# The sums of two group norms: VectorE's reductions, or matmuls with the values as weights

## The chip, the cores and the metric

The kernel runs on one core of one Trainium2 chip. The metric is device time in microseconds of one execution, from the runs' times; a profiled execution of the same kernel gives the trace. Engines have these names: PE is TensorE's matmul, PEld its weight load, DVE is VectorE, ACT is ScalarE, POOL is GpSimd, SP is the engine that issues the DMAs.

## The reference

For each of 16 samples (256 channels, 32 x 32 positions, f32), two layers are applied, each to a group norm of what came before, and each with a residual:

```python
    def _gn(v, G=16, eps=1e-5):
        B_, H_, W_, C_ = v.shape
        g = v.reshape(B_, H_, W_, G, C_ // G)
        m = jnp.mean(g, axis=(1, 2, 4), keepdims=True)
        s = jnp.var(g, axis=(1, 2, 4), keepdims=True)
        return ((g - m) / jnp.sqrt(s + eps)).reshape(v.shape)
    ...
    x = x + _L0_conv_ref(_gn(x), ...)
    x = x + _L1_conv_ref(_gn(x), ...)
```

The array given to `_gn` has the shape (16, 256, 32, 32). The norm takes its last axis, 32 wide, as channels: a group is two neighbouring columns of the 32 x 32 picture, over all 256 channels and all 32 rows, 16,384 numbers. There are 16 groups in a sample. Layer 0 is an attention block (4 heads of 32 on 1024 tokens, layer norms, a feed-forward part). Layer 1 is a gated state-space scan: 512 inner channels, 64 states each, a recurrence over 1024 steps, with projections, a short convolution and gates around it.

## The kernel before

**Layout.** A sample is held as two tiles of 128 channels x 1024 tokens, channels on the partitions. So a group of the norm is a set of columns, the same on each partition: column c belongs to group (c mod 32) // 2. A sum over a group needs a sum over columns within a partition and a sum over all partitions.

**The loop.** The recurrence is cut into units. A unit is one scan instruction on DVE (L922, 128 x 1024), and a sample has 256 of them (4 x 4 x 2 x 8), 4096 in all. With the scan of unit n the loop issues, in this order: the DMA that brings the operand `dub` of unit n + 6; POOL's product with `bt` for unit n + 4 (L905); a piece of `outputs` of the last block of eight units (PE L947 with 32 passes in a unit, ACT's copy L953 in every second one, PE L959 with 64 small passes and ACT's copy L963 in every eighth); the scan; `decay` of unit n + 2 (two PE matmuls L914 into a PSUM tile, then ACT's exponential L916 in place). The pool of decay tiles has two buffers, so a decay can be at most two units ahead. All engines work in program order, and the end of the kernel ties that order down for PE, ACT, DVE and POOL.

**The side work.** All else for the next sample (`first_norm`, `attention_layer`, `scan_inputs`) and the last step for the sample before (`gate_and_store`) is written as generators. After the decay of a unit, the loop takes as many steps from them as are due. A step yields its share; `rate_for` finds a rate so that a sample's shares, each at least one unit long if it is one or more, fill 247 units. A step with share 1.5 is thus followed by a pause of the larger of 1 and 1.5 / rate units. The shares of a sample add up to 271.9 where `gate_and_store` runs too. Sample 0 is prepared ahead of the loop, with no scan beside it, and the last 256 units have no sample to prepare.

**The norm.** `group_norm` (L258) is called twice for a sample: in `first_norm` (L360), in the first units of a sample's 256, and in `scan_inputs` (L610), some 160 units later. `sum_of` (L259) reduces a tile of 1024 columns to 16 sums on DVE (L261). `mean_of` (L263) adds the two tiles' sums over the partitions on PE with a matrix of 1/256 (L266), which leaves the result on every partition. DVE scales it (L278), subtracts it from both tiles (L280), and ACT squares them (L282). The same sums of the squares give the variance, on which ACT takes Ln and Exp (L291, L292; Ln takes the scale in), and DVE multiplies (L295). PSUM tiles of side work come from `psum`, two buffers in the pool `mm` while the scan runs.

Other lines that are spoken of: L435 is the attention's scores for the maxima, L445 a reduction of 64 columns, L465 the attention's values `v_ps` (128 x 128 f32 pieces of `xn` as weights), L491 and L503 the matmuls of the value stage, 32 steps of share 1.75 in a sample.

Of the kernel before, what the change touches and what calls it, by code (L numbers as in the profile page):

```python
# [11 lines left out]
F32 = mybir.dt.float32  # L12
BF16 = mybir.dt.bfloat16
AF = mybir.ActivationFunctionType
ALU = mybir.AluOpType
AX = mybir.AxisListType
# [3 lines left out]
P = 128  # L20
C = 256
KC = C // P
L = 1024
HL = 512
NG = 16
HEADS, DH = 4, 32
INNER = HEADS * DH
NJ = L // P
# [22 lines left out]
def attention_then_scan_kernel(  # L51
# [18 lines left out]
    nc = tc.nc  # L70
    B = x.shape[0]

    def pool(name, bufs, **kw):
        return ctx.enter_context(tc.tile_pool(name=name, bufs=bufs, **kw))

    const = pool("const", 1)
# [4 lines left out]
    small = pool("small", 2)  # L81
# [14 lines left out]
    def bank(src, name):  # L96
        return src.tile([P, HL], F32, name=name, tag="mm" if src is mm else "av")

    def free_bank(name):
        if spare:  # L100
            return spare.pop()
        if next(alone) is mm:
            return bank(mm, name)
        both = aps.tile([P, L], F32, name=name, tag="a")
        spare.append(both[:, hs(1)])
        return both[:, hs(0)]

    def psum(name, dims=P):
        return (bank(mm, name) if beside["scan"] else free_bank(name))[:dims]
# [7 lines left out]
    def work(name, n=L):  # L117
        return wide.tile([P, L + 2 + CONV], F32, name=name, tag="wide")[:, :n]
# [21 lines left out]
    ident = const.tile([P, P], F32, name="ident")  # L140
    make_identity(nc, ident)
    avg = const.tile([P, P], F32, name="avg")
    nc.vector.memset(avg, 1.0 / C)
    eps = const.tile([P, 1], F32, name="eps")
    nc.vector.memset(eps, 1e-5)

# [15 lines left out]
    for k in range(ND):  # L162
# [4 lines left out]
        for j in range(2):  # L167
# [3 lines left out]
                start=(j == 0), stop=(j == 1),  # L171
# [32 lines left out]
    t = work("ones_s")[:1]  # L204
# [3 lines left out]
    for k in range(KC):  # L208
        t = work("rel_s").rearrange("p (i j) -> p i j", j=32)
# [37 lines left out]
    def grouped(ap):  # L247
        return ap.rearrange("p (h g t) -> p h g t", g=NG, t=2)

    def over_group(s):  # L250
        return s.unsqueeze(1).unsqueeze(3).to_broadcast([P, L // (2 * NG), NG, 2])
# [4 lines left out]


    def group_norm(src, dst):  # L258
        def sum_of(part, s, k):  # L259
            view = part.rearrange("p (h g t) -> p g h t", g=NG, t=2)  # L260
            nc.vector.tensor_reduce(s[:, k, :], view, AX.XY, ALU.add)  # L261

        def mean_of(s, name):  # L263
            m = psum(f"{name}_ps")[:, :NG]
            for k in range(KC):
                nc.tensor.matmul(m, avg, s[:, k, :], start=(k == 0), stop=(k == KC - 1))  # L266
            return m

        per = C / (C * L / NG)
        s = small.tile([P, KC, NG], F32, name="gn_s", tag="gn_s")  # L270
        sum_of(src[0], s, 0)
        yield 1
        sum_of(src[1], s, 1)
        m = mean_of(s, "gn_m")
        yield 1
        s = small.tile([P, KC, NG], F32, name="gn_q", tag="gn_s")
        qs = []
        nc.vector.tensor_scalar(m, m, per, None, ALU.mult)  # L278
        for k in range(KC):
            nc.vector.tensor_tensor(grouped(dst[k]), grouped(src[k]), over_group(m), ALU.subtract)  # L280
            q = work("gn_sq")
            nc.scalar.activation(q, dst[k], AF.Square)  # L282
            qs.append(q)
            yield 1
        sum_of(qs[0], s, 0)
        yield 1
        sum_of(qs[1], s, 1)
        del qs, q
        v = mean_of(s, "gn_v")
        yield 1  # L290
        nc.scalar.activation(v, v, AF.Ln, bias=eps, scale=per)  # L291
        nc.scalar.activation(v, v, AF.Exp, scale=-0.5)  # L292
        yield 2.2
        for k in range(KC):
            nc.vector.tensor_tensor(grouped(dst[k]), grouped(dst[k]), over_group(v), ALU.mult)  # L295
            yield 0.6
# [53 lines left out]
    def first_norm(b):  # L350
        xs, tok = [], []
        kept = state[b]["kept"] = dram.tile([C, L], F32, name="kept", tag="kept")
        if "x" in state[b]:
            xs = state[b].pop("x")
        else:
            for go in fetches(xs, x[b]):
                go()
            yield 0.4
        gn = [work("gn") for _ in range(KC)]
        yield from along(group_norm(xs, gn), fetches(tok, pos))  # L360
        for k in range(KC):
            nc.vector.tensor_tensor(tok[k], tok[k], gn[k], ALU.add)
            nc.sync.dma_start(kept[ts(k, P), :], tok[k])
            yield 0.6
# [231 lines left out]
    def scan_inputs(b):  # L596
# [8 lines left out]
        for t in xp:  # L605
            nc.vector.memset(t[:, 0:1], 0.0)
            nc.vector.memset(t[:, L + 1 : L + 2], 0.0)
        rels = []
        yield from along(
            group_norm(xs, body),  # L610
            [partial(nc.sync.dma_start, st["xr"][ts(k, P), :], xs[k]) for k in range(KC)]
            + fetches(rels, rel) + bring,
# [387 lines left out]
    for n, (b, k, q, e, i) in enumerate(units):  # L1000
        at = n % UNITS
        if at == 0:
            parts = [prepare(b + 1)] if b + 1 < B else []
            total = steps * len(parts)
            if b > 0:
# [3 lines left out]
                total = total + GATE  # L1009
# [104 lines left out]
```

## Time and profile before

| | us |
|---|---|
| median of 3 runs | 13106.57 |
| lowest, highest | 13067.61, 13129.75 |
| the profiled execution | 13096.86 |
| its span, first to last instruction | 13095.1 |
| DVE busy | 11666.7 |
| POOL busy | 9815.4 |
| PE busy, PEld busy | 9717.3, 5456.0 |
| ACT busy | 7520.3 |
| DVE's scans L922 | 9215.1 |
| mean granted TensorE clock | 0.800 |

A row of the groups reads: line, engine, operation, output <- input by the program's names, shapes, count | busy us, mean ns of one | idle time of the engine ahead of them, and what ended most of it. The timeline gives start, length, engine, line and operation, with like neighbours merged and counted. An f32 matmul of the program stands as two matmul rows (passes) in the trace. A busy PE is not PE at its peak: matmuls overlap, and their ends are modelled.

### The profile page before, as it was taken

The numbers are of one execution on the slowest core, as the hardware profiler recorded it, in microseconds if no ns is written. First come the engines' busy times: TensorE is split into PE (matmuls) and PEld (weight loads), VectorE is DVE, ScalarE is ACT, GpSimd is POOL, SyncE is SP. The second block draws the span as 40 slices with busy tenths as digits, with TensorE's granted clock in tenths as the row PEclk, the third lists the DMA queues.
The fourth block names the chain that finished last, engine by engine and source line by source line (L and its number), as shares of the span: only waits on it lengthen the run. The fifth ranks groups of instructions, "written<-read, shape, count | busy, mean of one in ns | idle before, by whom it ended". The sixth has DMA issues, their size and how long they took to land.

```text
span 13095.1 us, 424083 instructions
## 1 busy us (share of the span) xinstructions
PE 9717.3 (74%) x186800; PEld 5456.0 (42%) x186800; DVE 11666.7 (89%) x7560; ACT 7520.3 (57%) x10421; POOL 9815.4 (75%) x4105
## 2 busy tenths in 40 slices
PE   6676876868778687786868767687686877868767
PEld 2344443444444344443444434444344444444445
DVE  3789999899999899988999898999989899889998
ACT  2465664655646556565665656566465664655654
POOL 0487876878778787786877768787687877878798
PEclk8887977879788697887879878797787977869755
DMA  1467666676666767666666666766667666676676
GB/s 52 165 220 238 208 218 218 220 243 201 221 216 219 235 200 233 216 220 231 211 224 218 213 223 213 236 210 219 218 218 234 205 218 217 218 236 204 227 248 231
DMA packets 1038401, 2820.10 MB, mean 215 GB/s; under 512 B 290370, under 2 KB 368451, under 8 KB 1036548
## 3 DMA queue, kind: packets, MB, share of 16 engines
q1 hardware_dynamic: 1036548, 2792.97, 64.6%
q8 instruction: 1459, 23.90, 0.7%
q14 instruction: 394, 3.23, 0.1%
HBM read 2513.82 MB, written 261.62 MB: 212 GB/s over the span
## 4 chain that ended last, share of the span: by engine, by line
DVE 36%; PE 31%; issue 13%; ACT 11%; DMA 6%; POOL 2%; SPq 1%; DVEq 0%; POOLq 0%; ACTq 0%
DVE h L922 25%; PE yb L947 6%; ACT a L916 5%; DVE mx L416 5%; PE a L914 5%; PE av L491 3%; PE g_ps L688 2%; DMA dub<-dus 2%; PE st_ps L503 2%; POOL dub L905 2%; PE z_ps L639 2%; PE yb L959 1%; PE m_ps L859 1%; PE qk_ps L403 1%; DVE u L674 1%
## 5 line engine op out<-in xcount | busy, mean ns | idle before, releaser
L905 POOL TENSOR_TENSOR dub<-dub,bt 128x1024 f32<-128x1024 f32 x4096 | 9810.6, 2417 | 3229.8 <-DMA dub<-dus 2896.6
L922 DVE TENSOR_TENSOR_SCAN h<-a,dub 128x1024 f32<-128x1024 f32 x4096 | 9215.1, 2278 | 752.0 <-ACT a L916 401.8
L916 ACT ACTIVATE a<-a,acol 128x1024 f32<-128x1024 f32 x4096 | 4462.8, 1090 | 3253.4 <-PE a L914 3206.7
L914 PE MATMUL a<-pieces,pick 48*128 48x512 bf16 x8192 | 1902.6, 455 | 2518.2 <-DVE h L922 2401.8
L947 PEld LDWEIGHTS yb<-h,cd 128*32 128x32 f32 x131072 | 2488.2, 128 | 2781.3 <-issue 1265.6
L947 PE MATMUL yb<-h,cd 128*32 128x64 f32 x131072 | 3255.8, 252 | 476.8 <-ACT y L953 325.2
L914 PEld LDWEIGHTS <-pick 48*128 48x128 bf16 x8192 | 603.3, 95 | 2915.4 <-issue 2467.5
L953 ACT COPY y<-yb 128x256 f32<-128x256 f32 x2048 | 763.6, 373 | 914.7 <-PE yb L947 907.5
L435 PE MATMUL s_ps<-k,q 32*64 32x512 f32 x4092 | 825.7, 619 | 95.5 <-DVE mx L416 95.0
L416 DVE TENSOR_REDUCE mx<-s_ps 128x1 f32<-128x512 f32 x1023 | 649.0, 681 | 15.5 <-PE s_ps L435 15.5
L491 PE MATMUL av<-pt,vv 128*64 128x512 f32 x2048 | 596.1, 662 | 3.0 <-ACT sums L480 1.7
L959 PE MATMUL yb<-turn,y 128*32 128x16 f32 x32768 | 591.4, 214 | 5.8 <-issue 4.9
L511 ACT ACTIVATE pt<-st_ps 128x512 f32<-128x512 f32 x1024 | 554.1, 599 | 60.9 <-PE st_ps L503 59.9
L959 PEld LDWEIGHTS yb<-turn,y 128*32 128x32 f32 x32768 | 573.8, 159 | 6.6 <-issue 5.2
L503 PE MATMUL st_ps<-sp 33*128 33x512 f32 x2048 | 561.8, 622 | 4.5 <-ACT pt L511 3.3
L963 ACT COPY yo<-yb 128x128 f32<-128x128 f32 x512 | 136.1, 266 | 587.8 <-PE yb L959 560.5
L688 PE MATMUL g_ps<-w,xp 128*128 128x256 f32 x1464 | 451.9, 447 | 0.0
L688 PEld LDWEIGHTS g_ps<-w,xp 128*128 128x128 f32 x1464 | 367.3, 326 | 65.5 <-issue 54.0
L435 PEld LDWEIGHTS s_ps<-k,q 32*64 32x64 f32 x4092 | 193.6, 131 | 440.8 <-DVE mx L416 421.1
L859 PE MATMUL m_ps<-w,xs 128*128 128x256 f32 x1024 | 317.5, 460 | 10.4 <-DVE xs L834 10.4
L674 DVE SCALAR_TENSOR_TENSOR u<-up,cwh,u 128x1024 f32<-128x1024 f32 x192 | 273.0, 1422 | 28.0 <-ACT u L666 27.7
L859 PEld LDWEIGHTS m_ps<-w,xs 128*128 128x128 f32 x1024 | 262.1, 328 | 55.9 <-issue 32.0
(177 smaller groups left out, 6690.8 us busy)
## 6 DMA issues: line engine op xcount, KB each, us to landing
dub<-dus SPq DMA_DIRECT2D x4096, 512.0 KB
dps<-pc SPq DMA_DIRECT2D x384, 128.0 KB
pieces<-dps SPq DMA_DIRECT2D x1024, 48.0 KB
xs<-in_x_dram SPq DMA_DIRECT2D x64, 512.0 KB
xs<-kept SPq DMA_DIRECT2D x64, 512.0 KB
zs<-z SPq DMA_DIRECT2D x64, 512.0 KB
ud<-u SPq DMA_DIRECT2D x64, 512.0 KB
dus<-du SPq DMA_DIRECT2D x64, 512.0 KB
```

The costliest lines, as they stand in the source:

```text
L416: nc.vector.tensor_reduce(mx[:, g, c, hf : hf + 1], s, AX.X, ALU.max)
L435: nc.tensor.matmul(waiting[g][0][ts(e, 64)], q4[r, ts(c, 64)], k4[r, hs(hf)], start=True, stop=True,)
L491: nc.tensor.matmul(av[ts(e, 2 * DH)], vv[j // (NJ // 2)][:, j % (NJ // 2), 2 * pair + e, :], pts[e], start=(j == 0), stop=(j == NJ - 1),)
L503: nc.tensor.matmul(s, ka[r, ts(j, P)], qa[r, hs(hf)], start=True, stop=True)
L688: nc.tensor.matmul(ps[:, ts(q, C)], xp[k][:, ds(first + t, P, 4)], wg_s[:, k, t, :], start=(k == 0 and t == 0), stop=False,)
L905: nc.gpsimd.tensor_tensor(v, v, blocks[units[n][0]]["bt"], ALU.mult)
L914: nc.tensor.matmul(a[:, hs(hf)], w, pieces[r], start=True, stop=True)
L916: nc.scalar.activation(a, a, AF.Exp, scale=acol[:, at : at + 1])
L922: nc.vector.tensor_tensor_scan(now["h", e][:, i, :], decays.pop(n), loaded.pop(n), 0.0, ALU.mult, ALU.add)
L947: nc.tensor.matmul(yb[ts(g, 32), ts(s, 64)], cd[:, at // 16, ts(c, 32)], hbuf[:, :, at : at + 8], start=(c == 0), stop=(c == 1),)
L953: nc.scalar.copy(y2[:, r], yb[:, :256])
L959: nc.tensor.matmul(some[ts(r, 32), x], y2[:, r, x:256:8], turn[:, x], start=True, stop=True)
```

## The change

The sum over the partitions comes first, and the sum over the columns second. `sum_of` issues eight matmuls on PE for a tile: 128 columns of values are the weights (128 x 128, f32), a column of ones is the moving side, and the result is one PSUM column with a sum over 128 channels for each of these 128 tokens. Two tiles give 16 such columns. `mean_of` reduces the 16 columns to one on DVE; now partition p holds the sum of all columns c with c mod 128 = p. A constant matrix `member` (128 x 16, 1/16384 where p belongs to the group) is multiplied by it, and one matmul with a matrix of ones brings the 16 means to every partition. The scalings of the mean and inside Ln fall away, since `member` holds them. Three constants are built ahead of the loop. Each half of a sum becomes a step of share 1.5, and `mean_of` a step of its own.

```diff
@@ -141,6 +141,15 @@
+    column = const.tile([P, 1], F32, name="column")
+    nc.vector.memset(column, 1.0)
+    every = const.tile([P, P], F32, name="every")
+    nc.vector.memset(every, 1.0)
+    member = const.tile([P, NG], F32, name="member")
+    nc.vector.tensor_reduce(
+        member, ident.rearrange("p (h g t) -> p g h t", g=NG, t=2), AX.XY, ALU.add
+    )
+    nc.vector.tensor_scalar(member, member, 1.0 / (C * L / NG), None, ALU.mult)
...
     def group_norm(src, dst):
-        def sum_of(part, s, k):
-            view = part.rearrange("p (h g t) -> p g h t", g=NG, t=2)
-            nc.vector.tensor_reduce(s[:, k, :], view, AX.XY, ALU.add)
-
-        def mean_of(s, name):
+        def sum_of(part, sums, k):
+            for j in range(NJ):
+                at = k * NJ + j
+                nc.tensor.matmul(
+                    sums[:, at : at + 1], part[:, ts(j, P)], column, start=True, stop=True
+                )
+
+        def mean_of(sums, name):
+            total = small.tile([P, 1], F32, name="gn_t", tag="gn_t")
+            nc.vector.tensor_reduce(total, sums, AX.X, ALU.add)
+            share = small.tile([P, NG], F32, name="gn_g", tag="gn_g")
+            nc.vector.tensor_scalar(share, member, total, None, ALU.mult)
             m = psum(f"{name}_ps")[:, :NG]
-            for k in range(KC):
-                nc.tensor.matmul(m, avg, s[:, k, :], start=(k == 0), stop=(k == KC - 1))
+            nc.tensor.matmul(m, every, share, start=True, stop=True)
             return m
 
-        per = C / (C * L / NG)
-        s = small.tile([P, KC, NG], F32, name="gn_s", tag="gn_s")
+        s = psum("gn_sum")[:, : KC * NJ]
         sum_of(src[0], s, 0)
-        yield 1
+        yield 1.5
         sum_of(src[1], s, 1)
+        yield 1.5
         m = mean_of(s, "gn_m")
         yield 1
-        s = small.tile([P, KC, NG], F32, name="gn_q", tag="gn_s")
         qs = []
-        nc.vector.tensor_scalar(m, m, per, None, ALU.mult)
...
+        s = psum("gn_sum")[:, : KC * NJ]
         sum_of(qs[0], s, 0)
-        yield 1
+        yield 1.5
         sum_of(qs[1], s, 1)
         del qs, q
+        yield 1.5
         v = mean_of(s, "gn_v")
         yield 1
-        nc.scalar.activation(v, v, AF.Ln, bias=eps, scale=per)
+        nc.scalar.activation(v, v, AF.Ln, bias=eps)
```

## The prediction

> **What bounds the kernel now.** I read the page first, its busy times and its chain.
>
> ```profile
> PE 9717.3 (74%) x186800; PEld 5456.0 (42%) x186800; DVE 11666.7 (89%) x7560; ACT 7520.3 (57%) x10421; POOL 9815.4 (75%) x4105
> ...
> DVE 36%; PE 31%; issue 13%; ACT 11%; DMA 6%; POOL 2%; SPq 1%; DVEq 0%; POOLq 0%; ACTq 0%
> ```
>
> VectorE is the fullest engine (89%, idle for 1428 us), but PE holds nearly as much of the chain. So the loop has to be read unit by unit (a unit: one scan and what is issued with it), in the stage that changes. Next the groups by line, shapes kept apart:
>
> ```profile
> L261 DVE TENSOR_REDUCE gn_q<-gn_sq 128x16 f32<-128x1024 f32 x64 | 76.4, 1196 | 0.0
> L261 DVE TENSOR_REDUCE gn_s<-xs 128x16 f32<-128x1024 f32 x64 | 75.8, 1204 | 7.1 <-DMA xs<-in_x_dram 7.1
> L266 PE MATMUL gn_m_ps<-gn_s,avg 128*128 128x16 f32 x128 | 37.6, 377 | 34.8 <-DVE gn_s L261 34.8
> L278 DVE TENSOR_SCALAR gn_m_ps<-gn_m_ps 128x16 f32<-128x16 f32 x32 | 5.3, 165 | 1.2 <-PE gn_m_ps L266 1.2
> ```
>
> The change removes the first two rows: 152.2 us, 1.2% of the span. It is little, so what comes in its place decides. The timeline of VectorE in a second norm:
>
> ```profile
> 12145.16 2.28 DVE L922 TENSOR_TENSOR_SCAN h<-a,dub 128x1024 f32<-128x1024 f32 x1
> 12147.35 1.19 DVE L261 TENSOR_REDUCE gn_s<-xs 128x16 f32<-128x1024 f32 x1
> 12148.46 2.28 DVE L922 TENSOR_TENSOR_SCAN h<-a,dub 128x1024 f32<-128x1024 f32 x1
> 12150.66 0.16 DVE L278 TENSOR_SCALAR gn_m_ps<-gn_m_ps 128x16 f32<-128x16 f32 x1
> ...
> 12161.92 6.64 DVE L922 TENSOR_TENSOR_SCAN h<-a,dub 128x1024 f32<-128x1024 f32 x3
> ```
>
> VectorE has no gap here: a unit with a reduction takes 3.30 us (12145.16 to 12148.46), three scans in a row take 6.64, so 2.21 each, and a reduction costs 1.1 us of the path, not 1.2. Last, PE in the same form as the new matmuls: v_ps (L465) has 128x128 f32 values as weights. Each f32 matmul is two passes in the trace (L465: 8 calls, 16 rows).
>
> ```profile
> 2287.34 0.61 PE L914 MATMUL a<-pieces,pick 48*128 48x512 bf16 x2 [0.56 <-DVE h L922]
> 2287.88 3.78 PE L465 MATMUL v_ps<-w,xn 128*128 128x128 f32 x16
> 2291.59 1.08 PE L947 MATMUL yb<-h,cd 128*32 128x64 f32 x32
> 2292.61 0.60 PE L914 MATMUL a<-pieces,pick 48*128 48x512 bf16 x2
> ...
> 2294.07 2.05 PE L465 MATMUL v_ps<-w,xn 128*128 128x128 f32 x16
> ```
>
> The same 16 passes take 3.78 us and 2.05 us. The windows tell why: the granted clock was 0.50 in the first and 1.00 in the second. And in the norms:
>
> ```profile
> 3095.00:3215.00 120.00, 107.38 (x2230) 51.24 (x2221) 106.40 (x48) 96.03 (x148) 109.94 (x48) 0.97 0.72 237
> 2818.00:2850.00 32.00, 15.26 (x278) 10.04 (x281) 29.79 (x18) 17.27 (x22) 32.00 (x15) 0.50 0.74 252
> 3311.00:3322.00 11.00, 7.86 (x180) 4.98 (x176) 11.00 (x13) 5.09 (x7) 4.45 (x3) 0.78 0.85 279
> 3322.00:3334.00 12.00, 6.13 (x137) 4.07 (x137) 11.97 (x9) 5.96 (x8) 10.53 (x5) 0.50 0.89 311
> ```
>
> (Columns: window, its length, busy us of PE, PEld, DVE, ACT, POOL, then clock, DMA share, GB/s.) The first is the attention's value stage, the second a first norm, the others a second norm. In the first norm, and in the second one from its 11th microsecond on, PE is busy for half of the time and at half clock.
>
> **The change part by part.** Two norms for each of 16 samples, two sums in each: 64 pairs of half-sums. Four pairs run in the prologue, 60 beside scans.
>
> Removed on VectorE: two reductions a pair, 2 x 1.1 = 2.2 us, 60 x 2.2 = 132 us, and 30 scalings L278 at 0.19 us (12150.66 to 12150.85), 6 us. Added on VectorE: in each pair a reduction of 16 columns and a scaling of 16, which no row has; L278's 0.16 bounds one from below, the reduction of 64 columns L445 (220 ns) from above: 0.36 for both, 22 us. If nothing waited, 132 + 6 - 22 = 116 us would be gained, 0.9%.
>
> Added on PE: 8 matmuls, 16 passes a half-sum, each with its own weights. The moving column is one wide; no row has that. From above L465 bounds it (0.213 us a pass at half clock, 3.4 us a half-sum; 0.112 and 1.8 at full). L266, with 16 columns and equal weights, is nearest: four passes take 1.17 us in 12148.03 to 12149.20, and a pair's ends there lie 0.21 us apart at half clock, as far as L465's. So a narrow moving side gains nothing: the weights set the pace. From below the 32-column passes of L947 (32 in 0.84 us) would give 0.42 us a half-sum. I take L465's pace, as L266 agrees.
>
> Who is behind these passes? PE's queue is in order: outputs of the last block (1.0 us at half clock), decay of the scan two units ahead (0.54), then the side step. A decay stuck behind a half-sum makes ACT's exponential late and then the scan; only two decays are ahead. From the end of a scan, at half clock (S0, S1 the two half-sums): decay 0.54, S0, outputs 1.0, decay 0.54, S1. VectorE, after two more scans (4.4), reaches the new small reduction and waits for S1: 0.3 to the end of the last pass (3.78 less 16 x 0.213 = 3.4, rounded down), 0.36 for both small operations. Behind it in VectorE's queue stand the next scans (two, 4.4), and POOL's buffers come free with these; the fourth one's decay is ready about then (outputs 1.0, then 1.75 from L914's start to the end of L916's exponential). The mean's matmul waits on PE for the small operations, with one matmul where there were two; the outputs and the decay of that unit are ahead of it, so nothing is late for it. The four scans end at 0.54 + 1.0 + 0.54 + 0.3 + 0.36 + 4.4 + S0 + S1 = 7.1 + S0 + S1. Before: 4 x 2.21 + 2.2 + 0.2 = 11.2. **The balance** is S0 + S1 = 4.1 us, 0.13 us a pass; the two measured paces, 0.112 and 0.213, lie on both sides of it. At full clock the first terms shrink to 6.6 and S0 + S1 = 3.5: 1.1 us gained a pair. At half clock 6.8: 2.7 lost. With one half-sum at each, 5.2: 1.1 lost.
>
> Which clock? L465 itself began at 0.50 and kept it for 3.3 us of dense passes; the next dense stretch, 3 us later, had 1.00. So I take the first half-sum at half clock and the second at full for the two pairs of a first norm and the second pair of a second norm (45 pairs, +1.1 each, 50 us). The first pair of a second norm has 0.78 already: near the balance, -0.3 each, 15 pairs, -5. **Sums: +45 us.**
>
> The Trainium skill (TensorE: Matmul & The Clock Gate, Part 1) says the clock is released after a busy window of about 3.4 us and falls back after an idle one, which fits the L465 rows; it does not say whether loading weights alone counts as busy. The same page (LDWEIGHTS) gives columns/1.2 ns, 107 ns for 128 columns, with no word of the clock; the L465 rows show that only at full clock. By that rule, as an estimate, S0 + S1 would be 3.4 us everywhere and the sums 0.7 us a pair, 42 us, faster.
>
> Moved: the step shares. A norm's shares grow by 4, so a batch's go from 271.9 to 279.9 in 247 units, and the rate from 1.179 to 1.238 (my working from the code). Steps of share 1.75 then come every 1.414 units instead of 1.484: 32 such in the value stage, 2.25 units fewer. That stage is full on all sides (107.4 PE, 109.9 POOL, 106.4 DVE of 120 us). A unit fewer takes 2.21 us of scan away but only 0.97 of PE (0.47 + 0.5 at full clock): 0 to 2.25 x 1.24 = 2.8 us a batch, I take 1.4, over 15 batches **+21 us** (0 to 42). In stages that VectorE fills, the denser steps cost nothing. The DMAs in the norms come with the same steps, at most a unit later, and are needed many units later: nothing.
>
> Prologue: the second half-sum can't start before its tile (25.38 us) and no scan hides it: 2 to 3.4 against 1.2 in four pairs, **+8 us**, with setup under 1.
>
> Sum: 45 + 21 + 8 = 74 on the profiled execution's 13096.9 (span 13095.1), which lies 10 us under the median of the runs, 13106.6: **13180**.
>
> **The rivals.**
> *Half clock throughout.* Passes with one column may not count as work for the clock; the norms' windows now stand at 0.50. 60 x 2.7 = 162, value stage 42, prologue 10, and up to 20 where the 64 small passes of L959 (1.17 us) follow a sum: 234 at most, 13340. Against: L465's change of clock.
> *Faster: full clock throughout.* If the passes keep to 0.11 us in all pairs, the decays are late by less than the removed reductions: 60 x -1.1 = -66, with nothing lost in the value stage and 4 in the prologue: 13045. At the pace of L947 it would be all of 116: 12990. It decides below 0.13 us a pass. Against: the windows at 0.50.
> *POOL and DMA set the pace.* In the second norm DMA is at 0.85 to 0.89 and POOL once waits 4.58 us for dub; in the first one POOL runs without a gap (32.00 of 32.00). If the scans wait there for POOL anyway, the sums cost 0, the value stage 10 and the prologue 8: 13125. Against: the timeline of the second norm, in which no scan waits for POOL.
>
> **How the numbers follow.** Forecast 0.40 (its own range 13130 to 13235), half clock 0.28, full clock 0.10, POOL and DMA 0.22. About 0.5% (13041 to 13172) is what a measurement of this kernel can tell from no change. Under it lies most of full clock: 0.08. Over it: half clock, and over half of the forecast: 0.51. The rest, 0.41, is within. The range goes from full clock's end, 13040, to 13345.
>
> **What would show it.** Right: L261's 1.2 us rows gone; 2048 passes in place of 256, 16 of them in 3.4 us where the clock is 0.50 and 1.8 where it is 1.00; the small reduction waiting 2 to 4 us for PE; more of the scan's wait for ACT's a; VectorE less busy by some 130 us and idle longer by more. Wrong: passes under 0.1 us at half clock, or scans that follow each other without a gap behind the sums; or a norm's stage that is as long as before while another stage has grown.

## The result, and the profile after

The changed kernel takes 20625.79 us (median of 4 runs, 20617.16 to 20649.53) against 13093.89 us (4 runs, 13067.61 to 13129.75) for the kernel before on the same chip: a ratio of 1.5752, with a 95% interval of 1.5716 to 1.5789. The prediction was 13180, with a range that ended at 13345. It was wrong, and not by a term of its sum: something happened that the sum did not hold.

The page of the changed kernel, with its busy times, its chain and the row of the scan (which was L922 and is L937 now; the lines below the norm have moved by 15):

```profile
PE 11861.3 (58%) x188720; PEld 6578.0 (32%) x188720; DVE 12059.0 (58%) x7532; ACT 7641.5 (37%) x10421; POOL 9771.5 (47%) x4105
...
DVE 42%; PE 32%; ACT 16%; issue 7%; DMA 1%; POOL 0%; DVEq 0%; SPq 0%; ACTq 0%; POOLq 0%
...
L937 DVE TENSOR_TENSOR_SCAN h<-a,dub 128x1024 f32<-128x1024 f32 x4096 | 9369.7, 2288 | 5512.4 <-ACT a L931 4639.0
```

The scans themselves are as long as before (2288 ns against 2278). What is new is the idle time ahead of them: 5512.4 us, and 4639.0 of it ended with ACT's `a`, the decay. The row of before:

```profile
L922 DVE TENSOR_TENSOR_SCAN h<-a,dub 128x1024 f32<-128x1024 f32 x4096 | 9215.1, 2278 | 752.0 <-ACT a L916 401.8 <-PE yb L947 156.3 <-POOL dub L905 110.6
```

So the idle time was 752.0 us there. The waits, as what waited for what, us in total, times and the longest, say who waits for whom:

```profile
ACT a L931 <- PE a L929: 9437.1, 3635, 7.6
...
PE a L929 <- DVE h L937: 8484.8, 3471, 15.5
...
DVE h L937 <- ACT a L931: 4639.0, 2663, 4.2
```

It is a ring: the exponential waits for PE's decay, the scan for the exponential, and PE's next decay for the scan (8484.8 us in 3471 waits). The timeline shows it best where nothing else runs. In this stretch of the last sample's units there is no side work and no sum, and still:

```profile
19704.07 2.29 DVE L937 TENSOR_TENSOR_SCAN h<-a,dub 128x1024 f32<-128x1024 f32 x1 [1.89 <-ACT a L931]
...
19706.41 0.61 PE L929 MATMUL a<-pieces,pick 48*128 48x512 bf16 x2 [2.56 <-DVE h L937]
...
19707.06 1.09 ACT L931 ACTIVATE a<-a,acol 128x1024 f32<-128x1024 f32 x1 [3.09 <-PE a L929]
...
19708.25 2.29 DVE L937 TENSOR_TENSOR_SCAN h<-a,dub 128x1024 f32<-128x1024 f32 x1 [1.89 <-ACT a L931]
```

The decay's matmul starts when a scan ends, the exponential follows it, and the next scan follows that: 4.18 us from scan to scan (19708.25 less 19704.07), 2.29 of scan and 1.89 of waiting. No decay is made ahead. The same place of the kernel before:

```profile
12595.59 17.91 DVE L922 TENSOR_TENSOR_SCAN h<-a,dub 128x1024 f32<-128x1024 f32 x8
```

Eight scans in 17.91 us, 2.24 each, with no gap. So units without a norm became slower too; no sum stands beside them that could do this. A second thing is seen in the sums themselves. The variance of the prologue's second norm, in the timeline and then in the windows (window, its length, busy us of PE, PEld, DVE, ACT, POOL, clock, DMA share, GB/s):

```profile
292.45 6.99 PE L271 MATMUL gn_sum<-column,gn_sq 128*128 128x1 f32 x32 [2.41 <-ACT gn_sq L295]
```

```profile
292.50:299.40 6.90, 6.90 (x32) 6.85 (x32) 0.00 (x0) 2.34 (x2) 0.00 (x0) 0.50 0.71 275
```

32 passes in 6.99 us, 0.218 each, back to back with PE busy for all of it, and the granted clock stays at 0.50 from end to end. The prediction expected it to be released in such a stretch.

The removed rows of 1.2 us are gone; in their place stand these two (the groups by line, shapes kept apart):

```profile
L279 DVE TENSOR_SCALAR gn_g<-member,gn_t 128x16 f32<-128x16 f32 x64 | 67.0, 1048 | 2.3
...
L277 DVE TENSOR_REDUCE gn_t<-gn_sum 128x1 f32<-128x16 f32 x63 | 10.7, 169 | 237.4 <-PE gn_sum L271 237.3
```

The reduction of 16 columns costs 0.17 us, but VectorE waits 237 us ahead of it. The scaling of 128x16 numbers costs 1.05 us, where the prediction took 0.36 for both operations.

**Where the decay tile went.** In the prologue, before any scan runs, `psum` takes its tiles from `free_bank`. It gives out a bank of `mm`, then the first half of a tile from the pool of decay tiles, then the second half of the same tile, which it keeps in the list `spare` until it is asked for: a cycle of three requests. Following the code, the kernel before makes 193 such requests in the prologue, 64 cycles and one: the list is empty when the loop begins. The change makes two more in each norm (`psum("gn_sum")`, where the sums had been in SBUF), four in the prologue: 197, 65 cycles and two. The last request takes a first half, and the second one stays in `spare`. Nobody asks for it as long as the loop runs, and so one of the two decay tiles stays taken.

### The profile page after: what moved, and what is told of

Read it like the earlier page. It is cut to its first block, busy times and chain, and to the rows that moved or that the text cites. A ratio compares the mean times of both kernels' runs of the same rounds, so it can differ in the third digit from the quotient of the medians.

```text
span 20615.4 us, 427971 instructions
## 1 busy us (share of the span) xinstructions
PE 11861.3 (58%) x188720; PEld 6578.0 (32%) x188720; DVE 12059.0 (58%) x7532; ACT 7641.5 (37%) x10421; POOL 9771.5 (47%) x4105
## 4 chain that ended last, share of the span: by engine, by line
DVE 42%; PE 32%; ACT 16%; issue 7%; DMA 1%; POOL 0%; DVEq 0%; SPq 0%; ACTq 0%; POOLq 0%
DVE h L937 37%; ACT a L931 13%; PE a L929 10%; PE s_ps L450 4%; PE yb L962 3%; PE av L506 3%; PE st_ps L518 2%; DVE mx L431 2%; PE gn_sum L271 2%; PE u_ps L675 1%; PE g_ps L703 1%; PE z_ps L654 1%; PE yb L974 1%; DMA dub<-dus 1%; PE m_ps L874 1%
## 5 line engine op out<-in xcount | busy, mean ns | idle before, releaser
L937 DVE TENSOR_TENSOR_SCAN h<-a,dub 128x1024 f32<-128x1024 f32 x4096 | 9369.7, 2288 | 5512.4 <-ACT a L931 4639.0
L929 PE MATMUL a<-pieces,pick 48*128 48x512 bf16 x8192 | 2181.6, 520 | 8566.8 <-DVE h L937 8484.8
L962 PEld LDWEIGHTS yb<-h,cd 128*32 128x32 f32 x131072 | 2954.5, 147 | 3068.6 <-issue 1963.6
L962 PE MATMUL yb<-h,cd 128*32 128x64 f32 x131072 | 3811.3, 282 | 42.3 <-ACT y L968 38.5
L929 PEld LDWEIGHTS <-pick 48*128 48x128 bf16 x8192 | 692.4, 97 | 9049.5 <-issue 7501.8
L450 PE MATMUL s_ps<-k,q 32*64 32x512 f32 x4096 | 912.0, 979 | 17.4 <-DVE mx L431 17.4
L506 PE MATMUL av<-pt,vv 128*64 128x512 f32 x2048 | 825.7, 897 | 2.8 <-ACT sums L495 1.6
L518 PE MATMUL st_ps<-sp 33*128 33x512 f32 x2046 | 805.2, 870 | 2.0 <-ACT pt L526 2.0
L675 PE MATMUL u_ps<-xp,w 128*128 128x512 f32 x508 | 353.0, 833 | 4.1 <-ACT u L681 4.1
L784 DVE SCALAR_TENSOR_TENSOR d_ps<-sp_s,d_ps 128x512 f32<-128x512 f32 x128 | 89.2, 697 | 382.8 <-ACT d_ps L780 382.8
```

The lines of the kernel that those rows point to most:

```text
L450: nc.tensor.matmul(waiting[g][0][ts(e, 64)], q4[r, ts(c, 64)], k4[r, hs(hf)], start=True, stop=True,)
L506: nc.tensor.matmul(av[ts(e, 2 * DH)], vv[j // (NJ // 2)][:, j % (NJ // 2), 2 * pair + e, :], pts[e], start=(j == 0), stop=(j == NJ - 1),)
L518: nc.tensor.matmul(s, ka[r, ts(j, P)], qa[r, hs(hf)], start=True, stop=True)
L929: nc.tensor.matmul(a[:, hs(hf)], w, pieces[r], start=True, stop=True)
L937: nc.vector.tensor_tensor_scan(now["h", e][:, i, :], decays.pop(n), loaded.pop(n), 0.0, ALU.mult, ALU.add)
L962: nc.tensor.matmul(yb[ts(g, 32), ts(s, 64)], cd[:, at // 16, ts(c, 32)], hbuf[:, :, at : at + 8], start=(c == 0), stop=(c == 1),)
```

## The experiments

Each ratio is to the kernel before as it ran in the same round, whose median lay between 13088 and 13102 us; so runs of different rounds are compared by their ratios too.

**e1: the half given back.** If this is the cause, one line after the prologue takes it away. In the kernel after:

```diff
     steps = list(prepare(0))
+    spare.clear()
```

> The changed kernel, with the list of spare PSUM halves emptied once, ahead of the loop. Theory A (a half left over from the prologue keeps one of the two decay tiles, so every scan waits for its own decay): the unit without side work falls from 4.18 us back to 2.2 us and the time to 13100 to 13400 us. What is then left over 13094 is the price of the sums themselves: 13180 by the terms of the prediction, about 13340 if the passes stay at half clock. Theory B (the passes of the sums block PE's queue and everything behind): stays above 20000, since no pass is taken away. Theory C (weight loads with a one-wide moving side pull PE's clock down everywhere): stays far above 13400 with a mean clock near 0.65.

Measured: 13280.85 us (13261.81 to 13306.18), ratio to before 1.014 (1.0124 to 1.0155). The page's row of its scans:

```profile
L937 DVE TENSOR_TENSOR_SCAN h<-a,dub 128x1024 f32<-128x1024 f32 x4096 | 9213.7, 2277 | 867.9 <-ACT a L931 450.4
```

7345 us of the change's 7532 are gone with one line that computes nothing. The rest (181 us, over the 13099.43 of the kernel before in this round) is what the sums and the shares cost, and is studied below.

**e2: the kernel before with one request more.** The other way round, with no sum on PE at all:

```diff
     steps = list(prepare(0))
+    nc.vector.memset(psum("odd")[:, :1], 0.0)
```

> The kernel before, with one more request for a PSUM bank at the end of the prologue (a memset of one column). Theory A: one half is left over here too, a unit of the last sample goes from 2.2 to 4.2 us, and the time to 20000 to 20700 us with VectorE's reductions in place and not one new matmul. Theories B and C: 13094 us, as before, within 0.5%.

Measured: 20468.72 us (20452.42 and 20485.02), ratio 1.5635 (1.5606 to 1.5663). Its row:

```profile
L922 DVE TENSOR_TENSOR_SCAN h<-a,dub 128x1024 f32<-128x1024 f32 x4096 | 9370.4, 2288 | 5629.5 <-ACT a L916 4597.9
```

It is the changed kernel's row within 3%. One request for a tile makes the kernel before slower by 56%. The two runs together show the cause: what decides is the half that the count of requests leaves over, not what is done with the tiles.

**e3: the shares alone.** The kernel before, with VectorE's sums, but with the steps and shares of the kernel after:

```diff
         sum_of(src[0], s, 0)
-        yield 1
+        yield 1.5
         sum_of(src[1], s, 1)
+        yield 1.5
```

(the same for the squares).

> The kernel before, with only the steps of the change: shares 1.5 for the half-sums and the mean as a step of its own, the sums on VectorE as before. No bank request is added. The prediction's term for the moved steps: +21 us, between 0 and 42. Theory A adds nothing to that; if the steps themselves were the cause of the large loss, the time would be far over 13400.

Measured: 13119.41 us (13096.34 to 13132.64), ratio 1.0012 (1.0002 to 1.0022), so 20 us. So of e1's 181 us some 160 are the sums' own. By stage, from the starts of the scans, mean over 14 batches, units counted within a sample's 256:

| us a batch | first norm (units 1-14) | 14-80 | values (80-140) | 140-158 | second norm (158-174) | 174-220 | 220-256 |
|---|---|---|---|---|---|---|---|
| before | 55.55 | 218.45 | 153.18 | 60.07 | 54.59 | 141.44 | 115.30 |
| e3 | 44.27 | 221.99 | 158.12 | 58.94 | 54.53 | 145.48 | 117.70 |
| e1 | 50.61 | 222.57 | 157.19 | 59.04 | 59.88 | 145.22 | 117.74 |

In e1 and e3 the first column holds no side work but the first norm; in the kernel before, the first operations of `gate_and_store` (4.9 us of work a batch and 5.3 of waits for `xs<-ud`) fall into it too. The norms of e1 are longer than those of e3 by 6.34 and 5.35 us, all other stages agree within 1 us. 11.69 us a batch over 15 batches are 175 us, against 161 between the medians. Each norm has two pairs of half-sums, so a pair costs 2.9 us.

**e5: half the passes.** From here on each kernel has e1's line. This one has four matmuls a half-sum in place of eight, so it leaves out half of the columns of each sum.

```diff
-            for j in range(NJ):
-                at = k * NJ + j
+            for j in range(NJ // 2):
+                at = k * NJ // 2 + j
```

> The first experiment's kernel with four matmuls a half-sum instead of eight: it leaves out half of the columns of each sum, so the norms are not the reference's. Theory Q (the passes at half clock hold up the decays): S0 + S1 falls from 7.1 to about 3.7 us, 3.4 a pair, some 200 us in 60 pairs, to about 13080, since that lies under the balance of 4.1. Theory F (the fixed part costs: the small operations, the waits for signals, the moved steps): less than 40 us of the 180 go, 13240 or more.

Measured: 13162.45 us (13155.9 to 13171.83), ratio 1.0064 (1.0048 to 1.008): 118 us less than e1 by medians, 100 by the ratios. It lies between the two theories. The price hangs on PE's passes, but is not in proportion: with half of them gone, e5 still lies 0.5% over e3. Something else grew, though: in e5's trace the scaling takes 2122 ns in the mean and 135.8 us in all, after 952 ns and 61.0 us in e1. No run tells how much of the 0.5% that is. The first norm falls from 50.61 to 47.63, the second from 59.88 to 55.18, where e3 has 54.53.

**e6: the same passes with 128 columns.** The moving side is the matrix of ones, 128 wide, in place of one column; 16 of the resulting columns are read.

```diff
-                    sums[:, at : at + 1], part[:, ts(j, P)], column, start=True, stop=True
+                    sums[:, at : at + P], part[:, ts(j, P)], every, start=True, stop=True
```

> The first experiment's kernel with 128 columns of ones as the moving side instead of one; each matmul writes 128 columns, of which only the first is kept. L465 showed the same pace for this form, 0.213 us a pass at half clock. Theory K (the clock is released by columns that stream through the array, not by loads of weights): the second half-sum now runs at full clock in most pairs, 1.9 instead of 3.57 us, and the time falls by 50 to 100 us, to 13180 to 13230. Rival (the stretch of passes is too short or too late for the clock anyway): the 16 passes keep 3.57 us, and 13280 stays.

Measured: 13156.38 us (13127.02 to 13176.76), ratio 1.0059 (1.0041 to 1.0076). More columns for PE, and yet 124 us less than e1 by the medians, 106 by the ratios, somewhat more than was expected. The rows of the sums' matmuls by line, with the shortest, median and longest in ns; first e1, then e6:

```profile
L271 PE MATMUL gn_sum<-column,gn_sq x1024: 352/352/374, 33.0 to 12363.3; 128*128 128x1 f32 x171
L271 PE MATMUL gn_sum<-column,xs x992: 250/352/374, 19.7 to 12343.6; 128*128 128x1 f32 x199
```

```profile
L271 PE MATMUL gn_sum<-every,gn_sq x1024: 274/377/582, 29.8 to 12176.2; 128*128 128x128 f32 x171
L271 PE MATMUL gn_sum<-every,xs x992: 274/275/582, 19.7 to 12158.6; 128*128 128x128 f32 x199
```

A record of 352 ns with one column, or 377 and more with 128, is one at half clock; 250 or 275 is one at full clock. In e1 none of the squares' passes is short, and 252 of all 2048; in e6 1190 are. The timeline of e6 in a second norm shows the release:

```profile
12169.36 3.78 PE L271 MATMUL gn_sum<-every,gn_sq 128*128 128x128 f32 x16
...
12174.41 2.05 PE L271 MATMUL gn_sum<-every,gn_sq 128*128 128x128 f32 x16
```

This is the prediction's picture, the first half-sum at half clock and the second at full. In e1 the same place has 3.57 us twice (12355.08 and 12360.13), both in windows with the clock at 0.50. The same is seen where PE has nothing else to do. The prologue's 32 passes, which took 6.99 us in the kernel after, in e6:

```profile
284.96 5.46 PE L271 MATMUL gn_sum<-every,gn_sq 128*128 128x128 f32 x32 [2.40 <-ACT gn_sq L295]
```

So here the width of the moving side decides whether a dense run of passes releases the clock. VectorE's wait for the sums falls from 165.3 us to 80.4.

The Trainium skill (TensorE: Matmul & The Clock Gate, Part 1) says that the clock is released after a busy window of about 3.4 us. The 6.99 us of passes in the kernel after were busy by the profile's rows and were not released: the page does not say what counts as busy, and in these runs loading 128 columns of weights for each single moving column did not.

**e4 and e8: the scaling.** The scaling on VectorE took 0.95 us a time in e1. e4 makes it a tensor_tensor, e8 gives it to ScalarE.

```diff
-            nc.vector.tensor_scalar(share, member, total, None, ALU.mult)
+            nc.vector.tensor_tensor(share, member, total.to_broadcast([P, NG]), ALU.mult)
```

```diff
-            nc.vector.tensor_scalar(share, member, total, None, ALU.mult)
+            nc.scalar.activation(share, member, AF.Identity, scale=total)
```

> The first experiment's kernel (spare halves emptied), with the scaling of the member matrix by a tensor_tensor with a broadcast column in place of the tensor_scalar, which took 0.95 us on average there, between 0.23 and 2.32. Theory P (the tensor_scalar on two SBUF operands has to wait until POOL's instruction ends, the tensor_tensor doesn't): about 0.2 us each, 64 times, and the time 20 to 45 us lower than the first experiment's, about 13245. Rival: the operation waits for the column that was written just before it; then it stays near 1 us and 13280.

> The first experiment's kernel (one-wide moving side, spare halves emptied) with the scaling of the member matrix on ACT instead of VectorE. In the traces 41 of 64 such VectorE instructions ran beside one of POOL's, and ended 0.03 us after it. Theory P2 (any VectorE instruction with two SBUF operands waits for POOL's running instruction): 61 us of VectorE go, and what of them was on the path, 30 to 60 us, comes off 13280. Rival (PE is late anyway in these units, so the wait only moves to the scan): under 15 us come off.

Measured: e4 13277.29 us, ratio 1.0154 (1.0135 to 1.0172); e8 13295.85 us, ratio 1.0152 (1.0135 to 1.0168). Neither gains anything over e1's 1.014. In e4 the instruction is nearly as slow as before, 869 ns in the mean, so it is not the form. In e1's trace 35 of the 64 scalings ended 0.03 us after an instruction of POOL that ran beside them, and took 1.55 us in the mean; the 29 others took 0.23. In e4's trace 41 ended so, with 1.26 us in the mean, and the 23 others took 0.18. In e8 they take 0.30 us on ScalarE, VectorE is rid of 61 us of them (its busy time falls by 35), and the time does not fall. The waits of e1 and of e8 for the sums:

```profile
DVE gn_t L277 <- PE gn_sum L271: 165.3, 49, 9.4
```

```profile
DVE gn_t L277 <- PE gn_sum L271: 163.6, 49, 8.3
```

They are the same, and VectorE's idle time as a whole rises from 1695.9 to 1716.9 us. The scaling was dear, but PE was late behind it: its price was not on the path.

**e7 and e11: the squares alone, in bf16.** VectorE keeps the sums of the mean, and the scaling that is left is e4's. ScalarE writes the squares as bf16, so that a matmul is one pass and not two; the variance comes from rounded squares. e11 has the scaling on ScalarE. A part of the edit, against the kernel before:

```diff
-            q = work("gn_sq")
+            q = ptp.tile([P, L], BF16, name="gn_sq", tag="pt")
             nc.scalar.activation(q, dst[k], AF.Square)
...
-        sum_of(qs[0], s, 0)
-        yield 1
-        sum_of(qs[1], s, 1)
...
+        columns_of(qs[0], s, 0)
+        yield 1
+        columns_of(qs[1], s, 1)
```

> The mean by VectorE as in the kernel before; only the sums of the squares on PE, with the squares written as bf16 by ACT, so that a matmul is one pass instead of two, and with a tensor_tensor for the scaling; spare halves emptied. One more step a norm. Theory Q: a half-sum of 8 passes of about 0.1 us holds PE for 0.9 us, less than the room beside a scan, so no decay is late; 2.2 - 0.4 = 1.8 us less a norm on VectorE, 30 norms, 54 us, of which the added step gives some back: about 13060. Theory F: the waits for the sums' signals take the gain, 13100 or more.

> The squares' sums in bf16 on PE, the mean on VectorE, as in the seventh run, with the scaling on ACT. The seventh run lost 144 us, though its passes took 0.04 to 0.1 us; its 32 scalings took 43 us and VectorE's other two-operand instructions 35 us more than before. Theory P2: 30 to 45 us come off 13232, so about 13190. If the loss is by where the moved steps fall, the rest stays.

Measured: e7 13231.85 us, ratio 1.0115 (1.0097 to 1.0134); e11 13196.23 us, 1.0073 (1.0057 to 1.0089). A quarter of e1's passes remains, and both are still slower than before, and than e6 in the medians. So e7's gain of 1.8 us a norm did not come. Here the scaling's move to ScalarE did pay, 36 us by the medians and 55 by the ratios, as was expected. What costs the rest (the half-sums that are neighbours again, the step more, the bf16 tiles from another pool) was not taken apart.

**e9, e10, e12: what is left.** e9 has e6's wide side and e8's scaling. e10 is e9 with shares of 1 behind the half-sums, e12 is e9 with a share of 2.5 behind the second half-sum, so that VectorE's reduction is issued about a unit later (the same for the squares; this raises a sample's shares to 283.9, not to the 281.9 of its expectation):

```diff
         sum_of(src[1], s, 1)
-        yield 1.5
+        yield 2.5
```

> Both edits that helped or should help: 128 columns of ones as the moving side (full clock for the second half-sum) and the scaling on ACT. Theory: the gains add, since one is PE's and the other VectorE's: 13156 less 30 to 70, 13085 to 13125, near the kernel before. Rival: same as the wide moving side alone, 13156.

> The same as the run of both edits, with shares of 1 instead of 1.5 behind the half-sums: these come in consecutive units in every norm, and the other steps are less dense (sum of shares 275.9 instead of 279.9). Theory (denser steps cost about 5 us for each unit of shares added): 10 us faster than with 1.5. Rival: slower by 10 to 30 us, since the half-sums then are always neighbours.

> The kernel of e9 (128 columns of ones as moving side, scaling on ScalarE, the half given back), with the share behind each second half-sum 2.5 instead of 1.5, so that VectorE's reduction of the 16 columns is issued about a unit later. The question is what is left of e9's +50 us over the kernel before (e3's shares cost 16 to 20, so some 30 are the sums' own). Theory L: VectorE's 89.9 us of waits for the sums (34 times) are late passes of PE that the reduction meets; a unit later they are done, and the scan in between does not wait itself: the wait falls under 30 us, the denser steps (a sample's shares go from 279.9 to 281.9) cost 5 to 15: 13090 to 13115, a ratio of 0.998 to 1.001 to the kernel before. Rival M: PE is late, not the reduction early; the scan in between then waits for its own decay, which stands in PE's queue behind the half-sum, and the wait only changes its name: gn_t's wait falls, the scan's for a and for yb rises by about as much, 13140 to 13165, 1.003 to 1.005.

Measured: e9 13146.84 us, ratio 1.0038 (1.0024 to 1.0052); e10 13317.26 us, 1.0167 (1.0149 to 1.0185); e12 13129.32 us, 1.0035 (1.0022 to 1.0048).

e9: 10 us less than e6 by the medians, 27 by the ratios, whose intervals overlap. The 30 to 70 us that were expected if the gains add were not reached.

e10: half-sums that are neighbours cost 170 us over e9, far more than was expected. VectorE's wait for the sums rises from 89.9 us to 195.3, and its waits for three transfers rise too (`xs<-ud` 37.5 to 91.3, `sums<-den` 17.7 to 63.9, `few<-den` 122.1 to 155.7). The kernel before, whose half-sums have shares of 1 too, has these three at 99.4, 47.7 and 154.9. The four are 239 us, more than the 184 by which its idle time grows; they were not told apart by a run.

e12: both theories failed by half. The wait for the sums did go, as L said:

```profile
DVE gn_t L277 <- PE gn_sum L271: 21.0, 4, 8.4
```

But the time did not, as M said (the ratio lies in M's range, the median below it), and not for M's reason alone: the scan's waits for `a` rose by 41 us and those for `yb` fell by 26, while waits of other steps came back, `xs<-ud` 37.5 to 74.5, `few<-den` 122.1 to 151.8, `sums<-den` 17.7 to 44.8, `f_ps` 6.6 to 33.2, `m_ps` 11.3 to 31.2. In all VectorE is idle for 1551.4 us, after 1556.1. A step that is moved by a unit moves all behind it; that this is why the other waits came back is argued, not shown. No version with sums on PE was faster than the kernel before.

## Why the prediction was wrong, by its own steps

**The step that failed** is the one that asked who is behind the passes: "only two decays are ahead". The prediction used the two decay tiles as a given, and priced the change only in the units of the norms. It counted instructions, DMAs and waits that the change moves, and never the requests that it makes for PSUM, though the diff puts `gn_sum` there. That the tiles of the prologue come from the same pool as the decays was in the code that the change calls (`psum`, `free_bank`), and no row of the profile of before shows it: there the list happened to be empty. The traces show the step's price, 1.89 us of waiting a unit where there is no side work, and e2 shows it in all: 56%. No rival held it either.

**The clock** ("the first half-sum at half clock and the second at full") failed for one-wide passes and holds for 128-wide ones (e6). L465, from which it was taken, has 128 moving columns. "The weights set the pace" was right, but the weights did not set the clock. The rival of half clock throughout was nearly right here: 1796 of e1's 2048 passes are at half clock.

**The pace of a pass** was right: 0.218 us at half clock, against the 0.213 taken. A narrow moving side gained nothing.

**The formula of the four scans** came near at its half-clock value: 2.7 us lost a pair, and 2.9 measured between e1 and e3, with the small reduction waiting 3.4 us a time (165.3 us in 49 waits). But the wait is not only where the formula has it. In e1's timeline VectorE has a gap ahead of the scan behind the second half-sum:

```profile
12360.13 3.57 PE L271 MATMUL gn_sum<-column,gn_sq 128*128 128x1 f32 x16
...
12363.63 1.08 PE L962 MATMUL yb<-h,cd 128*32 128x64 f32 x32
...
12364.88 2.29 DVE L937 TENSOR_TENSOR_SCAN h<-a,dub 128x1024 f32<-128x1024 f32 x1 [6.03 <-PE yb L962]
```

In this place it is the scan that waits, and not for a decay but for the outputs behind the sums: by the code, a new block's scan writes a buffer that these outputs still read. This wait was not in the formula; e6 and e3 have less of it (175 and 82 us in all, e1 198). Since e1 has 116 us more of it than e3, and dearer small operations besides, that 2.7 and 2.9 lie so close is in part luck.

**The small operations**, 0.36 us for both, were off: 0.17 and 0.95. The bound from below was L278, whose input lies in PSUM; the scaling's two inputs lie in SBUF. Rows that show the difference were in the profile of before:

```profile
L362 DVE TENSOR_TENSOR xs<-xs,gn 128x1024 f32<-128x1024 f32 x32 | 67.2, 2136 | 0.0
L280 DVE TENSOR_TENSOR gn<-xs,gn_m_ps 128x1024 f32<-128x1024 f32 x32 | 38.6, 1209 | 0.5
```

L362 adds two SBUF tiles in 2136 ns in the mean, 3.19 us in the 15 cases beside POOL and 1.21 in the 17 others; L280, of the same size with one input in PSUM, takes 1209. With one-wide passes the error cost nothing that could be measured (e8).

**The shares**, +21 us, came out at 20 (3 to 29 by the interval of e3), but by another way than given. The value stage did become longer, by 4.9 us a batch in place of 1.4, and units 174 to 256 by 6.4; units 1 to 80 became shorter by 7.7. The first column of the table falls by more, 11.3, because `gate_and_store`, with 10.2 us of work and waits, begins behind it in e3. Why the denser steps help there and cost elsewhere was not taken apart. The agreement of the net is in part luck.

**The prologue**, +8, is +10: the first scan starts at 445.9 us in e1, after 435.5.

Had the buffer been given back, the time was e1's 13281, inside the range and over its forecast, 59 us under the half-clock rival's 13340. The rival of POOL and DMA as the pace fell: e6 changes only PE's matmuls, and with them its clock, and the time follows.

**What stays open**: where the last 0.38% of e9 and 0.35% of e12 lie. e3's shares explain 0.12% of e9's. The two traces of e9 and e3 lie 13 us apart. In them VectorE is busy for 122 us less (11578.6 after 11700.4) and idle for 134 us more, spread over many waits; e9's two norms are longer than e3's by 6.4 us a batch (49.60 and 55.58), its units 14 to 140 shorter by 5.6, and its first scan starts 9 us later (443.3 after 434.4). No run isolates one of these.

## What to carry to other kernels

Before pricing a new use of a shared pool, count the requests and see in what state the count leaves the allocator, for the phases behind it too; a tile that one phase takes and does not give back costs the next phase its overlap, and no row of the old profile can say so. Work that moves from a full engine to one that stands in the same ring of waits in order is worth its time only as far as the ring has slack: here, in e1, 2.2 us less on VectorE in a pair bought 7 us of PE ahead of the next decay and the next outputs. A duration is carried over from a row only if its operands lie where the new ones will, and a granted clock only if the moving side is as wide.

## What the runs showed of the hardware that was not expected

Passes with 128 columns of f32 weights and one moving column did not release TensorE's clock: 32 of them ran back to back for 6.99 us at 0.50. The same 32 with 128 moving columns took 5.46 us, and in a norm beside scans of e6 the second of two runs of 16 with 128 moving columns, 5 us after the first, ran at full clock (2.05 us after 3.78). Wider matmuls made e1's kernel faster by 0.8%.

A small VectorE instruction with two inputs in SBUF waited for the POOL instruction that was running: in e4, 41 of 64 ended 0.03 us after POOL's and took 1.26 us in the mean, and the others took 0.18. The Trainium skill (SBUF — State Buffer, Who interferes with whom) says that a VectorE instruction with two SBUF inputs contends with one of POOL that reads SBUF, that the shared ports are an exclusive lock, and that the order of issue decides who blocks; the trace agrees, with POOL's products, about 2.4 us long, as the holder.
